# A shared expert's second product with its weights standing and 512 tokens moving, turned back in the final sums

## The chip, the cores and the metric

The kernel runs on one core of a Trainium2 chip. The metric is device time in microseconds (us), the median of several runs. PE is TensorE, DVE VectorE, ACT ScalarE, POOL GpSimd, and SP the engine whose queue issues most of the DMAs. An f32 matmul shows in the profile as two instructions.

## The reference

The input x has 8 sequences of 512 tokens with 128 features. A layer norm modulated by a conditioning vector is followed by four Mamba2 layers and a residual sum with a gate; a second modulated layer norm is followed by a mixture of experts. Only the mixture matters here:

```python
normed = hidden_states * rsqrt(mean(hidden_states**2) + 1e-08) * norm_weight
shared = maximum(normed @ sw1 + sb1, 0.0) @ sw2 + sb2     # 128 -> 512 -> 128, all tokens
...                                                       # 8 experts of that size, 2 a token
return shared + routed
x = x + gb * ffn(h)                                       # gb: one row of 128 a sequence
```

## The kernel before, in words

The first two thirds are the Mamba layers. While the last scan steps drain, streams of small steps are merged by a planner (`arrange`, L724): every step names an engine, a cost in us, what it needs and gives, and a PSUM bank that it takes or drops; the planner picks the step that could start first, and the order in which it picks them is the order in every engine's queue. The streams are the scan's lanes, the routing of four sets of two sequences (`rejoin`, L372), the rows' scatter into lists by expert (`send`), the shared expert's products on PE (`shared_products`, L595) and its evictions on ACT (`shared_copies`, L621), and the first 17 tiles of the routed experts.

The shared expert works by sequence b. Four first products (L601) have a block of `sw1` as weights and the sequence's 512 tokens, features on the partitions, moving; each fills a bank and leaves it with bias and relu (L632) as a part of `hds[b]`, hidden units on the partitions. The second product (L613) has 128 tokens of `hds` as weights and a block of `sw2` moving, so that its result has tokens on the partitions: for each of four token blocks s four products over the hidden units k add up in a quarter of one bank. Each s is one planner step of cost 0.9. A copy on ACT (L636) puts the bank into `accs[b]`, which lies in a tile of the Mamba layers' states (shown as `h`).

The routed experts then go through 39 tiles of 256 rows, the last 22 of them in a loop written out by hand: load weights and rows of tile j+3 (`fetch`), hidden products of tile j+1 (L1563), turn of tile j+2 (L1551), second products of tile j (`combine`, L1581), weighing (`weigh_results`, L1593 and L1595 on DVE), scatter of the results into `yg` (L562). Every pass of this loop also takes two steps of the folds. `fold(b)` has four: load the gate row `gb` to all partitions (L1510, SP's queue), add the bias `b2` to `accs[b]` (L1512), multiply by `gb` (L1514), add to `xs[b]`, the residual (L1516).

When the last scatter is done, two rows a token are read back from `yg` on SP's and ACT's queues (L1709). For each sequence PE adds both in a bank by products with the identity as weights (L1715, L1716), DVE multiplies by `gb` (L1718) and adds to `xs[b]` (L1721), and SP stores the result (L1722).

Of the kernel before, what the change touches and what calls it, by code (L numbers as in the profile page):

```python
# [8 lines left out]
F32 = mybir.dt.float32  # L9
I32 = mybir.dt.int32  # L10
AF = mybir.ActivationFunctionType
# [4 lines left out]
P = 128  # L16
# [38 lines left out]
def adaln_mamba_moe(  # L55
# [27 lines left out]
    nc = tc.nc  # L83
    B, L, DM = x.shape
# [4 lines left out]
    NC = L // Q  # L89
# [4 lines left out]
    FK = FH // P  # L94
# [39 lines left out]
    ident = const.tile([P, P], F32, name="ident")  # L134
# [115 lines left out]
    hTs, hp, xp, xs = {}, {}, {}, {}  # L250
# [3 lines left out]
    fp = ctx.enter_context(tc.tile_pool(name="fp", bufs=1))  # L254
# [4 lines left out]

    rwT = fp.tile([P, E], F32, name="rwT")  # L260
    b1 = fp.tile([P, E1, FK], F32, name="b1")
    b2 = fp.tile([P, DM], F32, name="b2")
    rank = fp.tile([P, E], F32, name="rank")
    below = fp.tile([P, P], F32, name="below")
    base = fp.tile([P, E], F32, name="base")
# [25 lines left out]
    def prepare_experts(pool):  # L291

        pm = pbank("pmods")
        nc.tensor.matmul(pm[:B, : 4 * DM], sc, wm[:, 2 * DM :], start=True, stop=True)
        pv = pm[:B, : 4 * DM].rearrange("p (k d) -> p k d", d=DM)
        mod, mag = (pool.tile([P, NH, Q], F32, tag="dV", name=n)[:, :4, :DM] for n in ("mod", "mag"))
        yield
        nc.scalar.activation(mag[:B, :2, :], pv[:, 0:4:3, :], AF.Abs)
        nc.scalar.copy(mod[:B, 1, :], pv[:, 1, :])
        nc.scalar.activation(mod[:B, 2, :], pv[:, 2, :], AF.Copy, bias=1.0)  # L300
        nc.vector.tensor_scalar(mag[:B, 2:, :], pv[:, 0:4:3, :], 0.0, 2.0, ALU.is_ge, ALU.mult)

        nc.gpsimd.iota(rank, pattern=[[-1, E]], base=E, channel_multiplier=0, **exact)
        nc.gpsimd.iota(base, pattern=[[ER, E]], base=0, channel_multiplier=0, **exact)
        yield
        nc.vector.tensor_scalar_max(mag[:B, :2, :], mag[:B, :2, :], 0.25)
        for k in range(2):
            nc.vector.scalar_tensor_tensor(
                mod[:B, 3 * k, :], mag[:B, 2 + k, :], -1.0, mag[:B, k, :], ALU.add, ALU.mult
            )  # L310
        nc.gpsimd.tensor_sub(below, upto, ident)
        nc.gpsimd.iota(tok, pattern=[[L, 2], [1, NC]], base=0, channel_multiplier=NC, **exact)
        yield
        nc.vector.tensor_mul(mod[:B, 0, :], mod[:B, 0, :], fw[:B])
        yield
        nc.sync.dma_start(mods, mod[:B])
        yield
        with nc.allow_non_contiguous_dma(reason="small parameters, laid out once"):
            nc.sync.dma_start(rwT, router_w.rearrange("e d -> d e"))
            nc.sync.dma_start(b1[:, :E, :], eb1.rearrange("e (k p) -> p e k", p=P))  # L320
            nc.sync.dma_start(b1[:, E, :], sb1.rearrange("(k p) -> p k", p=P))
        nc.sync.dma_start(b2, sb2.partition_broadcast(P))
        yield

    hTx = {}
# [27 lines left out]
    def one(engine, cost):  # L353
        return ((engine, cost),)
# [227 lines left out]
    def pbank(name):  # L582
        pool, tag = pools[pick[0]], "p"
        if spare:
            pool, tag = spare[0]
            spare.append(spare.pop(0))
        return pool.tile([P, 512], F32, tag=tag, name=name)


    accs, w12 = {}, []  # L590

    home = {b: g for g, seqs in enumerate(sets) for b in seqs}
    hds, phs, pes = {}, {}, {}

    def shared_products():  # L595

        for b in range(B + 1):
            for k in range(FK if b < B else 0):
                yield one("PE", 0.87), (("routed", home[b]), ("weights", 0)), ("ph", b, k), ("ph", b, k), None
                phs[b, k] = ph = pbank(f"phs{b}_{k}")  # L600
                nc.tensor.matmul(ph[:, :L], w12[0][:, k * P : (k + 1) * P], hTx[b], start=True, stop=True)  # L601
            for s in range(NC if b else 0):
                yield (
                    one("PE", 0.9),
                    (("hidden", b - 1),),
                    ("pe", b - 1) if s == NC - 1 else None,
                    ("pe", b - 1) if s == 0 else None,
                    None,
                )
                if s == 0:  # L610
                    hd, pes[b - 1] = hds.pop(b - 1), pbank(f"pes{b - 1}")
                for k in range(FK):
                    nc.tensor.matmul(  # L613
                        pes[b - 1][:, s * DM : (s + 1) * DM],
                        hd[:, k, s * P : (s + 1) * P],
                        w12[1][:, k * P : (k + 1) * P],
                        start=(k == 0),
                        stop=(k == FK - 1),
                    )

    def shared_copies():  # L621

        for b in range(B + 1):
            for k in range(FK if b < B else 0):
                needs = (("ph", b, k),)
                if k == 0 and b < XB:
                    needs = (("ph", b, k), ("out", (NL * B - XB + b + 1) * NC - 1))
                yield one("ACT", 0.69), needs, ("hidden", b) if k == FK - 1 else None, None, ("ph", b, k)
                if k == 0:
                    hds[b] = xbp.tile([P, NX, L], F32, tag="xbc", name=f"hds{b}")  # L630
                ph = phs.pop((b, k))
                nc.scalar.activation(hds[b][:, k, :], ph[:, :L], AF.Relu, bias=b1[:, E, k : k + 1])  # L632
            if b:
                yield one("ACT", 0.6), (("pe", b - 1),), None, None, ("pe", b - 1)
                accs[b - 1] = hp[(b - 1) // 2][:, (b - 1) % 2]
                nc.scalar.copy(accs[b - 1].rearrange("p s d -> p (s d)"), pes.pop(b - 1))  # L636

    tab, done = {}, []

# [113 lines left out]
    with ExitStack() as actx:  # L753
# [530 lines left out]
        for t in range(-NC * LEAD - EARLY, TAIL):  # L1284
            p = t + NC * LEAD
# [23 lines left out]
            u, s = divmod(t, NC)  # L1309
# [194 lines left out]
    gbs = {}  # L1504
    fgb = ctx.enter_context(tc.tile_pool(name="fgb", bufs=B))

    def fold(b):

        gbs[b] = fgb.tile([P, DM], F32, tag="gb", name=f"gb{b}")
        nc.sync.dma_start(gbs[b], mods[b, 3].partition_broadcast(P))  # L1510
        yield
        nc.vector.tensor_add(accs[b], accs[b], b2.unsqueeze(1).to_broadcast([P, NC, DM]))  # L1512
        yield
        nc.vector.tensor_mul(accs[b], accs[b], gbs[b].unsqueeze(1).to_broadcast([P, NC, DM]))  # L1514
        yield
        nc.vector.tensor_add(xs[b], xs[b], accs[b])  # L1516

    xts, w1x, w2x, b2x, rows_in, hdx, pts, pxs, ys = ({} for _ in range(9))

# [151 lines left out]
    def hidden(j):  # L1671
        pick[0] = "P"
        for half in range(2):
            hidden_product(j, half)
            hidden_relu(j, half)

    with tc.manual_schedule():
        for js in ((J0, J0 + 1), (J0 + 2,)):
            for rest in [fetch(j) for j in js]:
                rest()  # L1680
        for j in (J0, J0 + 1):
            turn(j)
            turned_copy(j)
        hidden(J0)
        folding = [fold(b) for b in range(B)]
        for j in range(J0, NT):
            if j + 3 < NT:
                fetch(j + 3)()
            if j + 1 < NT:
                hidden(j + 1)  # L1690
            if j + 2 < NT:
                turn(j + 2)
                turned_copy(j + 2)
            pick[0] = "D"
            combine(j)
            weigh_results(j)
            send_results(j)
            for _ in range(2):
                if folding and not step(folding[0]):
                    del folding[0]  # L1700

        pick[0] = "P"
        y1, y2 = {}, {}
        for b in range(B):
            both = xbp.tile([P, NX, L], F32, tag="xbc", name=f"y{b}") if b % 2 == 0 else both
            for c, (eng, y) in enumerate(((nc.sync, y1), (nc.scalar, y2))):
                y[b] = both[:, 2 * (b % 2) + c, :]
                r = c * T + b * L
                eng.dma_start(  # L1709
                    y[b].rearrange("p (s d) -> p s d", d=DM),  # L1710
                    yg[r : r + L, :].rearrange("(p s) d -> p s d", s=NC),
                )
        for b in range(B):
            sum2 = pbank(f"sum{b}")
            nc.tensor.matmul(sum2, ident, y1[b], start=True, stop=False)  # L1715
            nc.tensor.matmul(sum2, ident, y2[b], start=False, stop=True)  # L1716
            y = y1[b].rearrange("p (s d) -> p s d", d=DM)
            nc.vector.tensor_mul(  # L1718
                y, sum2.rearrange("p (s d) -> p s d", d=DM), gbs[b].unsqueeze(1).to_broadcast([P, NC, DM])
            )  # L1720
            nc.vector.tensor_add(xs[b], xs[b], y)  # L1721
            nc.sync.dma_start(out[b].rearrange("(s p) d -> p s d", p=P), xs[b])  # L1722
# [51 lines left out]
```

## Time and profile before

| what | value |
|---|---|
| median of 3 runs | 1024.13 us (1022.54 to 1024.15) |
| the profiled execution's own time | 1026.45 us |
| its span, first to last instruction | 1024.7 us |
| PE busy | 907.9 us, 89% |
| DVE, ACT, POOL busy | 80%, 75%, 81% |
| mean granted TensorE clock | 0.952 |
| first products of the shared expert (L601) | 64 instructions, 739.6 to 830.1 us |
| second products (L613) | 256 instructions, 748.4 to 837.6 us |
| copies of their results (L636) | 8, median 0.586 us |
| folds (L1512, L1514, L1516) | 3 x 8, 0.683, 0.683 and 0.692 us, 913.5 to 974.0 us |
| final sums (L1715, L1716) | 32 instructions, from 1003.3 us |

The profile gives instructions by line, engine and tile. Its first block cuts the span into 40 slices and shows each engine's busy tenths; its chain of waits goes back from the last instruction to what released it. PE's instructions are pipelined, so that their durations overlap: an instruction's real share of the time is seen from the chain, where a group's length is divided by its count. PEld are the weight loads, which run beside the products.

### The profile page before, as it was taken

The numbers are of one execution on the slowest core, as the hardware profiler recorded it, in microseconds if no ns is written. First come the engines' busy times: TensorE is split into PE (matmuls) and PEld (weight loads), VectorE is DVE, ScalarE is ACT, GpSimd is POOL, SyncE is SP. The second block draws the span as 40 slices with busy tenths as digits, with TensorE's granted clock in tenths as the row PEclk, the third lists the DMA queues.
The fourth block names the chain that finished last, engine by engine and source line by source line (L and its number), as shares of the span: only waits on it lengthen the run. The fifth ranks groups of instructions, "written<-read, shape, count | busy, mean of one in ns | idle before, by whom it ended". The sixth has DMA issues, their size and how long they took to land.

```text
span 1024.7 us, 21895 instructions
## 1 busy us (share of the span) xinstructions
PE 907.9 (89%) x7284; PEld 677.1 (66%) x7284; DVE 821.4 (80%) x2012; ACT 767.1 (75%) x1765; POOL 831.5 (81%) x847
## 2 busy tenths in 40 slices
PE   4669899999999999999999999777687999999976
PEld 2336676676777666777767677566455678888862
DVE  3879989899999899999899999687765665457744
ACT  4897899999999999999999989864585533333320
POOL 8768899999999999999999999676868775445550
PEclk9888999999999999999999999998787899999997
DMA  6142455665766656653434434540011257778737
GB/s 124 5 157 69 149 168 159 184 184 177 201 198 186 180 170 187 186 175 119 141 114 135 134 115 141 181 152 25 32 32 44 69 151 209 217 220 230 226 113 246
DMA packets 134304, 151.23 MB, mean 148 GB/s; under 512 B 22568, under 2 KB 106696, under 8 KB 134192
## 3 DMA queue, kind: packets, MB, share of 16 engines
q1 hardware_dynamic: 127184, 137.91, 45.2%
q0 software_dynamic: 4672, 9.42, 2.7%
q10 hardware_dynamic: 2336, 2.50, 0.8%
q8 instruction: 58, 0.95, 0.4%
q14 instruction: 54, 0.44, 0.1%
HBM read 120.07 MB, written 29.71 MB: 146 GB/s over the span
## 4 chain that ended last, share of the span: by engine, by line
PE 45%; ACT 17%; POOL 16%; DVE 9%; DMA 7%; issue 5%; SPq 1%; POOLq 0%; ACTq 0%; DVEq 0%
PE pe L1581 5%; POOL dV L1022 5%; PE px L839 4%; PE ph L1563 4%; PE py L1163 4%; DMA rows<-xg 3%; PE po L1216 3%; PE pz L844 3%; PE py L1153 3%; POOL dV L1030 3%; PE phs L601 3%; PE py L1101 2%; PE py L1110 2%; POOL xd L1077 2%; ACT xbc L873 2%
## 5 line engine op out<-in xcount | busy, mean ns | idle before, releaser
L860 DVE SCALAR_TENSOR_TENSOR xbc<-px,cw,xbc 128x511 f32<-128x511 f32 (+2 forms) x384 | 284.1, 741 | 13.1 <-ACT xbc L850 10.1
L1022 POOL TENSOR_TENSOR dV<-dV,cum 128x1024 f32<-128x1024 f32 (+1 forms) x128 | 232.5, 1817 | 7.6 <-DMA dV<-crow 7.4
L1092 DVE TENSOR_TENSOR dV<-dV,ptx 128x1024 f32<-128x1024 f32 x128 | 155.2, 1213 | 17.9 <-ACT xT L1070 11.4
L1030 POOL TENSOR_SCALAR_AFFINE_SELECT dV<-dV 128x1024 f32<-128x1024 f32 x128 | 141.1, 1102 | 1.2
L562 POOL DMA_INDIRECT yg<-y,ix x78 | 81.0, 1038 | 68.7 <-DVE y L1595 52.2
L1077 POOL TENSOR_TENSOR xd<-xT,dt 128x512 f32<-128x512 f32 (+1 forms) x128 | 120.6, 942 | 18.2 <-ACT xT L1070 17.8
L1043 ACT ACTIVATE dV<-dV 128x1024 f32<-128x1024 f32 (+1 forms) x128 | 129.2, 1010 | 3.7 <-POOL dV L1030 3.3
L850 ACT ACTIVATE xbc<-px,cbias,cw 128x512 f32<-128x512 f32 x128 | 100.0, 782 | 6.3 <-PE px L839 5.4
L839 PE MATMUL px<-hT,Wi 128*128 128x512 f32 x192 | 99.5, 600 | 0.0
L1101 PEld LDWEIGHTS py<-xbc,st 128*128 128x128 f32 x384 | 57.1, 195 | 61.9 <-issue 25.5
L1574 ACT ACTIVATE hd<-ph,bs 128x256 f32<-128x256 f32 x78 | 32.8, 471 | 80.1 <-PE ph L1563 79.2
L1216 PE MATMUL po<-Wo,g 128*128 128x128 f32 x512 | 89.2, 297 | 0.0
L562 POOL DMA_INDIRECT xg<-row,ix x64 | 63.5, 993 | 27.0 <-issue 16.1
L1163 PE MATMUL py<-dV,xd 128*32 128x128 f32 x2048 | 83.8, 282 | 0.0
L1153 PEld LDWEIGHTS py<-xbc,dg 128*128 128x128 f32 x512 | 76.4, 195 | 5.2
L1153 PE MATMUL py<-xbc,dg 128*128 128x128 f32 x512 | 79.8, 279 | 0.0
L1216 PEld LDWEIGHTS po<-Wo,g 128*128 128x128 f32 x512 | 69.1, 196 | 13.1 <-issue 12.9
L1110 PE MATMUL py<-xd,xT 128*128 128x256 f32 x192 | 61.1, 401 | 16.6 <-issue 8.1
L1581 PE MATMUL pe<-w,hd 128*128 128x128 f32 x624 | 75.7, 275 | 0.0
L1563 PE MATMUL ph<-xt,w 128*128 128x256 f32 x312 | 73.9, 380 | 1.4 <-ACT xt L1555 1.4
L1101 PE MATMUL py<-xbc,st 128*128 128x128 f32 x384 | 61.3, 283 | 13.6 <-DVE rg L1223 6.8
L1581 PEld LDWEIGHTS pe<-w,hd 128*128 128x128 f32 x624 | 72.7, 192 | 0.1
(264 smaller groups left out, 2225.2 us busy)
## 6 DMA issues: line engine op xcount, KB each, us to landing
dV<-crow SPq DMA_DIRECT2D x128, 512.0 KB
w<-in_L_ffn_ew_dram SPq DMA_DIRECT2D x78, 256.0 KB
xg<-blank SPq DMA_DIRECT2D x64, 260.0 KB
ecum<-crow SPq DMA_DIRECT2D x256, 48.0 KB
rows<-xg SPq DMA_DIRECT2D x39, 130.0 KB
b<-in_L_ffn_eb_dram SPq DMA_DIRECT2D x39, 64.0 KB
x<-in_L_attn_x_dram SPq DMA_DIRECT2D x8, 256.0 KB
md<-mods SPq DMA_DIRECT2D x8, 256.0 KB
```

Source lines behind the costliest of these rows:

```text
L562: i = nc.gpsimd.indirect_dma_start(out=to, out_offset=bass.IndirectOffsetOnAxis(ap=ix, axis=0), in_=of, in_offset=None)
L839: nc.tensor.matmul(px[v, k][:, :L], Wi[l][:, c0 : c0 + P], hT[v], start=True, stop=True)
L860: nc.vector.scalar_tensor_tensor(xbc[v][:, k, d:], px[v, k][:, : L - d], cw[:, l, k, KT - 1 - d : KT - d], xbc[v][:, k, d:], ALU.mult, ALU ...
L1022: nc.gpsimd.tensor_tensor(dV[i][:, :w], dV[i][:, :w], cums[g][:, h0 : h0 + w].unsqueeze(2).to_broadcast([P, w, Q]), ALU.subtract,)
L1030: nc.gpsimd.affine_select(out=dV[i], in_=dV[i], pattern=[[0, NH], [1, Q]], compare_op=ALU.is_ge, fill=-1e30, base=0, channel_multiplier=-1,)
L1043: nc.scalar.activation(dV[i][:, :w], dV[i][:, :w], AF.Exp)
L1077: nc.gpsimd.tensor_mul(xds[i][:, :w], xv.unsqueeze(1).to_broadcast([P, w, NH, HD]), dts[g][:, :w, h0 : h0 + NH].unsqueeze(3).to_broadcast( ...
L1092: nc.vector.tensor_mul(Ms[i], Ms[i], pg.pop(i).unsqueeze(1).to_broadcast([P, NH, Q]))
L1101: nc.tensor.matmul(py[i][:, k, :], st[i - 1][:, k * P : (k + 1) * P], xbc[u][:, NB + 1, t], start=(k == 0), stop=True, skip_group_check=True,)
L1153: nc.tensor.matmul(py[i][:, k, :], dg[l][:, k, :], xbc[u][:, k, t], start=False, stop=True, skip_group_check=True,)
L1216: nc.tensor.matmul(pp[:, c * DM : (c + 1) * DM], g[:, k, :], Wo[l][:, k, :], start=(k == 0), stop=(k == NB - 1))
L1581: nc.tensor.matmul(pe[:, s, :], hd[:, k, s * P : (s + 1) * P], w2[:, k, :], start=(k == 0), stop=(k == FK - 1))
```

## The change

The second product of the shared expert swaps its operands. A block of `sw2` is the weights, and a part k of the hidden tile moves, 512 tokens at once; four such products add up over a whole bank. The result has features on the partitions and tokens along the free axis. The bias `sb2` is then one value a partition, and is added in the eviction, which becomes an activation (Identity with a bias). `fold(b)` keeps only the load of the gate row. In the final sums the result is turned back: four products a sequence, each with 128 tokens of `accs[b]` as weights and the identity moving, open the bank to which the two identity products of before add the routed rows. The turns of sequences 0 and 1 stand ahead of the first sum, and those of b+2 behind the sum of b.

```diff
-    b2 = fp.tile([P, DM], F32, name="b2")
+    b2 = fp.tile([P, 1], F32, name="b2")
...
-        nc.sync.dma_start(b2, sb2.partition_broadcast(P))
+        nc.sync.dma_start(b2, sb2.rearrange("(p o) -> p o", o=1))
...
-            for s in range(NC if b else 0):
+            for k in range(FK if b else 0):
                 yield (
                     one("PE", 0.9),
                     (("hidden", b - 1),),
...
-                for k in range(FK):
-                    nc.tensor.matmul(
-                        pes[b - 1][:, s * DM : (s + 1) * DM],
-                        hd[:, k, s * P : (s + 1) * P],
-                        w12[1][:, k * P : (k + 1) * P],
-                        start=(k == 0),
-                        stop=(k == FK - 1),
-                    )
+                nc.tensor.matmul(
+                    pes[b - 1][:, :L],
+                    w12[1][:, k * P : (k + 1) * P],
+                    hd[:, k, :],
+                    start=(k == 0),
+                    stop=(k == FK - 1),
+                )
...
-                accs[b - 1] = hp[(b - 1) // 2][:, (b - 1) % 2]
-                nc.scalar.copy(accs[b - 1].rearrange("p s d -> p (s d)"), pes.pop(b - 1))
+                accs[b - 1] = hp[(b - 1) // 2][:, (b - 1) % 2].rearrange("p s d -> p (s d)")
+                nc.scalar.activation(accs[b - 1], pes.pop(b - 1), AF.Identity, bias=b2)
...
         nc.sync.dma_start(gbs[b], mods[b, 3].partition_broadcast(P))
         yield
-        nc.vector.tensor_add(accs[b], accs[b], b2.unsqueeze(1).to_broadcast([P, NC, DM]))
-        yield
-        nc.vector.tensor_mul(accs[b], accs[b], gbs[b].unsqueeze(1).to_broadcast([P, NC, DM]))
-        yield
-        nc.vector.tensor_add(xs[b], xs[b], accs[b])
...
+        def shared_rows(b):
+            sums[b] = pbank(f"sum{b}")
+            for s in range(NC):
+                nc.tensor.matmul(
+                    sums[b][:, s * DM : (s + 1) * DM], accs[b][:, s * P : (s + 1) * P], ident, start=(s == 0), stop=False
+                )
+
+        for b in range(2):
+            shared_rows(b)
         for b in range(B):
-            sum2 = pbank(f"sum{b}")
-            nc.tensor.matmul(sum2, ident, y1[b], start=True, stop=False)
+            sum2 = sums[b]
+            nc.tensor.matmul(sum2, ident, y1[b], start=False, stop=False)
             nc.tensor.matmul(sum2, ident, y2[b], start=False, stop=True)
+            if b + 2 < B:
+                shared_rows(b + 2)
```

More of the change, by code (lines that the diff above doesn't have):

```diff
@@ L605, in shared_products @@
                     (("hidden", b - 1),),
-                    ("pe", b - 1) if s == NC - 1 else None,
-                    ("pe", b - 1) if s == 0 else None,
+                    ("pe", b - 1) if k == FK - 1 else None,
+                    ("pe", b - 1) if k == 0 else None,
                     None,
                 )
-                if s == 0:
+                if k == 0:
                     hd, pes[b - 1] = hds.pop(b - 1), pbank(f"pes{b - 1}")
-                for k in range(FK):
-                    nc.tensor.matmul(
-                        pes[b - 1][:, s * DM : (s + 1) * DM],
-                        hd[:, k, s * P : (s + 1) * P],
-                        w12[1][:, k * P : (k + 1) * P],
-                        start=(k == 0),
-                        stop=(k == FK - 1),
-                    )
+                nc.tensor.matmul(
[5 more added lines that the diff above has]
+                )
     def shared_copies():
@@ L1712, in adaln_mamba_moe @@
                 )
+        sums = {}
+        def shared_rows(b):
[6 more added lines that the diff above has]
+            shared_rows(b)
         for b in range(B):
-            sum2 = pbank(f"sum{b}")
-            nc.tensor.matmul(sum2, ident, y1[b], start=True, stop=False)
+            sum2 = sums[b]
+            nc.tensor.matmul(sum2, ident, y1[b], start=False, stop=False)
             nc.tensor.matmul(sum2, ident, y2[b], start=False, stop=True)
+            if b + 2 < B:
+                shared_rows(b + 2)
             y = y1[b].rearrange("p (s d) -> p s d", d=DM)
```

## The prediction

> **What bounds the kernel now.** I read the page first, for where TensorE (PE) is full, then the chain of waits piece by piece for the three stretches that the change touches, then the waits and the busy time by windows inside each.
>
> ```profile
> PE   4669899999999999999999999777687999999976
> PEclk9888999999999999999999999998787899999997
> ```
>
> A slice is 25.6 us. PE is full to about 640 us, thins out while the scan drains, the rows are routed and the shared expert runs (739 to 838 us), is full again through the routed experts (839 to 993 us), and ends in a short tail. The change takes work from the second and third stretch and puts work into the last. The chain of waits at the end of the shared expert:
>
> ```profile
> 823.04 2.68 PE pes L613 x24
> ...
> 827.28 3.44 PE phs L601 x8
> 830.72 7.16 PE pes L613 x64
> ```
>
> Columns are start, length, instruction and count; an f32 matmul is two instructions. A first product (L601, 512 columns moving) costs 3.44/8 = 0.430 us an instruction, a second product (L613, 128 columns) 7.16/64 = 0.112 us. The time follows the columns: 4 x 0.112 = 0.448 against 0.430. The stretch of routed experts, by windows before, during and after the folds:
>
> ```profile
> 860.00:910.00 50.00, 47.69 (x322) 42.83 (x322) 25.03 (x87) 15.87 (x37) 24.90 (x26) 1.00 0.74 214
> 910.00:976.00 66.00, 63.46 (x438) 57.33 (x437) 47.82 (x140) 22.12 (x51) 36.92 (x32) 1.00 0.79 226
> 976.00:993.00 17.00, 16.27 (x117) 15.03 (x116) 9.07 (x33) 4.78 (x11) 7.90 (x10) 1.00 0.44 126
> ```
>
> The second number is the window's length, the third PE's busy time, the fifth VectorE's (DVE). DVE goes from 50% to 72% where the folds run, and PE stays at 95%, 96%, 96%: PE paces this stretch with and without them. The tail by the chain:
>
> ```profile
> 998.84 4.43 DMA y<-yg
> 1003.32 2.08 PE sum L1715 x2
> 1005.40 1.71 PE sum L1716 x2
> ...
> 1018.26 0.86 PE sum L1715 x2
> 1019.12 0.87 PE sum L1716 x2
> 1020.01 0.70 DVE y L1718
> 1020.74 0.69 DVE x L1721
> ```
>
> Once the first rows have landed, every piece is PE until 1019.99. The waits from 994 us on say the same, seen from DVE, and show the free gap ahead:
>
> ```profile
> DVE y L1718 <- PE sum L1716: 15.6, 8, 12.7
> ...
> PE sum L1715 <- DMA y<-yg: 9.8, 1, 9.8
> ```
>
> DVE waits for PE before each of its 8 products; PE waits for a load once, 9.8 us, before the first sum, and never again. PE's granted clock is the third number from the right here:
>
> ```profile
> 998.00:1000.00 2.00, 0.00 (x0) 0.00 (x0) 0.00 (x0) 0.00 (x0) 0.00 (x0) 0.61 0.28 53
> ...
> 1003.00:1004.00 1.00, 0.68 (x1) 0.50 (x2) 0.00 (x0) 0.00 (x0) 0.00 (x0) 0.50 0.96 348
> ...
> 1008.00:1009.00 1.00, 1.00 (x2) 0.33 (x2) 0.56 (x1) 0.00 (x0) 0.00 (x0) 0.65 1.06 397
> 1009.00:1010.00 1.00, 1.00 (x4) 0.44 (x3) 0.29 (x1) 0.00 (x0) 0.00 (x0) 1.00 1.05 393
> ```
>
> The gap halves the clock near 998.4, and it is whole again near 1008.7, so the tail's first 5.4 us run at half speed.
>
> **The change, part by part.**
>
> *Second product.* Per batch 16 matmuls of 128 columns become 4 of 512: 32 instructions of 0.112 us (3.58) become 8 of 0.430 us (3.44), 0.14 us less. Columns streamed stay 2,048, and the full clock is granted wherever L613 runs. Five of the eight groups lie on the chain of waits (at 768, 798, 823 to 827, and two from 830.7); behind the other three PE sits idle for 1.5 us or more, waiting for the routing. So I take 5 x 0.14 = 0.7 us gained, bounds 0 and 8 x 0.14 = 1.1. The steps for the planner keep their number (4), engine, cost (0.9), needs and bank, so its order stays; the new products could also start on a first part of the hidden tile, but they stand behind later first products anyway.
>
> The Trainium skill speaks for the change here: "TensorE: Matmul & The Clock Gate", section "Back-to-back issue gap", gives about 81 ns a matmul at 128 columns and 131 ns at 512 in a stream of weight loads and matmuls. As an estimate from that page, 256 x 0.081 = 20.7 us would become 64 x 0.131 = 8.4, five eighths of the difference is 7.7 us, and with 48 x 0.081 = 3.9 us in the tail and 0.2 for the evictions the sum would be a gain of 3.6 us. Both figures lie under this trace's 112 and 430 ns, and their ratio of 1.6 stands against 3.8; the trace decides.
>
> *Eviction.* The copy (L636, 0.586 us) becomes an activation with a bias. The nearest row is L632, same shape, from PSUM, with a bias: 0.687. The chain passes the copy twice: at 802.29, where the next set's squares queue behind it on ScalarE, and at 837.96, where the first routed tile's turned copy does, with PE waiting. 2 x 0.1 = 0.2 us lost, bounds 0 and 8 x 0.1 = 0.8.
>
> *Folds.* 24 DVE passes of 0.68 to 0.69 us (16.5 us) go. Nobody waits on the chain for them: L1593 starts within a microsecond or two of the products that it reads, and the 16 tiles with folds (L1593 at 912.60 to 976.11) take 3.97 us each, the 14 before (845.43 to 900.45) 3.93. I take nothing. At most, PE's waits for rows in that stretch go (0.41 + 1.01 + 0.98 = 2.4 us at 914.7, 942.4 and 966.1); but the stretch before has such waits too (0.72, 0.66, 0.56), without folds. What is late next there is PE itself, at 3.73 us a tile where it never waits (L1593 at 892.91 and 896.64, for one). The 8 loads of gb (64 KB each, 0.43 us to issue on SP's queue) remain, one per tile instead of one every second; SP issues its loads about two tiles ahead, and nothing but those loads queues behind. The bias load moves from 64 KB to 512 bytes early on SP's queue, hidden by 700 us.
>
> *Final sums.* Per batch 4 matmuls of 128 x 128, 8 instructions, each with weights of its own. The row with that shape and that change of weights is L1581, on the chain at 3.59/32 = 0.112 us, so 8 x 0.112 = 0.9 us a batch; from below 0.430/4 = 0.107 by the columns of L601, from above 0.112 + 0.192 = 0.304 if no weight load overlapped (the mean weight load of L1581). I take L1581, where the loads overlap. Batches 0 and 1 need only what lay ready since 838 us and banks whose last reader ended by 991, so they run from 993.5 to 995.3, inside the 9.8 us wait: free, and if that cover were gone they would cost 1.8. The other six stand between the sums, where PE never waits: 6 x 0.9 = 5.4 us, bounds 5.2 and, unoverlapped, 14.6. PE's extra wait is for a bank: batch b+2's turn needs the bank of sum b-1, read by DVE 0.3 + 0.7 us after that sum, while PE needs 1.7 us for sum b; so it waits for nothing, and only the next sums queue behind it.
>
> *Clock in the tail.* The half-speed time is a stretch of time, not of work: what is added lands at full clock behind it. PE's gap shrinks to 8.0 us, and the clock fell 4.9 us into the gap, so it falls again. Rise and fall are 3 x 3.4 us apart, as if in steps of 3.4; a start at another point of a step moves the rise by up to 1.7 us either way, worth half of it, 0.85 us.
>
> *Sum.* 5.4 - 0.7 + 0.2 = +4.9 us. The profiled execution took 1026.45 (span 1024.7 and 1.75 around it) and would take 1031.3. It lies 2.3 above the median of 1024.13, so on the runs I add the same: **1029.0**.
>
> **The rivals.**
>
> *Faster: the second product was held by its weight loads.* L613 has 256 loads of 0.192 us, 49 us in all, and only 64 remain. If the new passes took no more than a 256-column one (L1563, 1.73/8 = 0.216 us), a group would fall from 3.58 to 1.73, five groups save 9.2 us, and 5.4 + 0.2 - 9.2 = -3.6 gives 1020.5. It decides once a pass is under (5 x 3.58 - 5.6 - 2.0)/40 = 0.26 us. Against: L601 is that very shape, and takes 0.430.
>
> *No change: the tail hides it.* If the early turns of batches 0 and 1 held the clock up past 1003.3, the half-speed loss of 5.4/2 = 2.7 us would go: 4.9 - 2.7 = +2.2, 1026.3, and with the folds' 2.4 us gained on top -0.2, 1023.9. For it: 1.8 us more of work sits in the gap. Against: 8.0 us without work remain, and the clock fell after 4.9.
>
> *Much slower: weight loads in the tail don't overlap.* 48 x 0.304 = 14.6 in place of 5.4 gives +14.1, 1038.2. Against: L1581 and the old L613 alternate loads and passes in the same way at 0.112.
>
> *It doesn't do what it says.* If the planner placed the new products elsewhere, the routing would shift; its inputs are equal, so I give this nothing of its own.
>
> **How the numbers follow.** My forecast 0.86, faster 0.04, no change 0.07, much slower 0.03. A difference of 0.2% is 2.05 us, about what a measurement of this kernel can tell from no change. The forecast's own range: below, 5.2 - 1.1 - 0.85 = 3.2, and half of the folds' 2.4 off, 2.0: 1026.1; above, 5.4 + 0.85 + 0.8 = 7.1: 1031.2. That range leaves out most of the rivals' 0.14 and a little more, so I keep it. A hundredth of the forecast's chance falls under 2.05 us. Slower 0.88, same 0.08, faster 0.04.
>
> **What would show it.** Right: L613 as 64 instructions at 0.43 us on the chain; the three fold lines gone and tiles still near 3.95 us apart; 16 short instructions near 994; PE without a gap from the first sum to the last, that stretch 22.0 us long instead of 16.7; nothing between the last sum and the end changed. Wrong: PE waiting within the sums for loads or banks (the tail had another bound), the last routed product well before 992 us (the folds cost more than nothing), passes of L613 under 0.4 us, or full clock at the first sum.

## The result, and the profile after

The changed kernel took 1029.21 us (median of 11 runs, 1026.81 to 1034.88), the one before, run beside it, 1024.62 (11 runs): ratio 1.0047, 95% interval 1.0027 to 1.0067, or 2.8 to 6.9 us more. The forecast was 1029.0 and slower. Its profiled execution took 1031.35 us, span 1029.6; the sum had said 1031.3.

Later runs fell on several chips. On two of those the kernel before took some 30 us more and the changed kernel some 23, and there the changed kernel was level or faster (0.9982 and 0.9968). That is the part nobody had forecast; it has a section of its own.

The chain of waits at the end of the shared expert, after (start, length, instruction and count):

```profile
822.02 2.58 PE pes L612 x6
...
826.13 3.43 PE phs L601 x8
829.56 6.88 PE pes L612 x16
```

A second product is now 8 instructions in 3.44 us, where it was 32 in 3.58: 0.430 us a pass, as a first product. The routed stretch by windows (length, then busy time of PE, weight loads, DVE, ACT, POOL, then clock, DMA share, GB/s):

```profile
860.00:910.00 50.00, 47.28 (x324) 42.92 (x323) 24.80 (x88) 15.62 (x36) 24.98 (x27) 1.00 0.78 219
910.00:976.00 66.00, 63.70 (x441) 58.09 (x440) 33.84 (x118) 22.30 (x51) 30.92 (x33) 1.00 0.80 227
```

The folds are gone from DVE (33.84 us in the second window, 47.82 before), and PE is busy for 63.70 us of 66 instead of 63.46. The tail by the chain:

```profile
998.38 4.32 DMA y<-yg
1002.74 2.08 PE sum L1720 x2
1004.82 1.71 PE sum L1721 x2
1006.52 1.71 PE sum L1712 x8
1008.23 0.95 PE sum L1720 x2
...
1020.48 0.89 PE sum L1712 x8
...
1023.95 0.87 PE sum L1721 x2
1024.85 0.70 DVE y L1725
```

L1712 are the turns (8 instructions a sequence). PE has no hole from 1002.74 to 1024.82, 22.08 us against 16.67 before: 5.41 more, with 5.4 forecast. The turns of one sequence take 0.89 us, those in the half-speed part 1.71. From 996 us on DVE still waits for PE before each product, and PE for a load once:

```profile
DVE y L1725 <- PE sum L1721: 20.9, 8, 12.5
...
PE sum L1720 <- DMA y<-yg: 7.9, 1, 7.9
```

### The profile page after: what moved, and what is told of

Read it like the earlier page. It is cut to its first block, busy times and chain, and to the rows that moved or that the text cites. A ratio compares the mean times of both kernels' runs of the same rounds, so it can differ in the third digit from the quotient of the medians.

```text
span 1029.6 us, 21609 instructions
## 1 busy us (share of the span) xinstructions
PE 914.0 (89%) x7156; PEld 667.0 (65%) x7156; DVE 807.0 (78%) x1988; ACT 767.2 (75%) x1765; POOL 824.6 (80%) x847
## 4 chain that ended last, share of the span: by engine, by line
PE 49%; ACT 17%; POOL 13%; DVE 8%; DMA 7%; issue 4%; SPq 1%; POOLq 0%; DVEq 0%; ACTq 0%
PE px L838 5%; PE pe L1575 5%; PE py L1162 4%; PE po L1215 4%; POOL dV L1021 4%; PE ph L1557 4%; DMA rows<-xg 3%; PE pz L843 3%; PE py L1152 3%; PE py L1100 3%; PE py L1109 3%; PE phs L601 2%; POOL dV L1029 2%; DVE dV L1091 2%; ACT xbc L872 2%
## 5 line engine op out<-in xcount | busy, mean ns | idle before, releaser
L562 POOL DMA_INDIRECT yg<-y,ix x78 | 74.6, 957 | 75.7 <-DVE y L1589 58.9
```

Of the source, the lines that this page charges most:

```text
L562: i = nc.gpsimd.indirect_dma_start(out=to, out_offset=bass.IndirectOffsetOnAxis(ap=ix, axis=0), in_=of, in_offset=None)
```

## The experiments

Durations of the tail run from the start of the first sum to the end of the last, in the profiled execution. Repeated runs of one kernel lie 5 to 14 us apart, so a term under 2 us is read from the trace, and the ratio only bounds the whole.

**No turns.** The two early calls and the one behind the sums are out.

```diff
-        for b in range(2):
-            shared_rows(b)
...
-            if b + 2 < B:
-                shared_rows(b + 2)
```

> The changed kernel without the 32 turns: the shared expert's result is computed and evicted and left out of the output. If PE paces the tail, all of the loss goes: the stretch from the first sum to the last falls from 22.1 to 16.7 us and the time to 0.5 us under that of the kernel before, 0.9995 of it. Rival, the loss came from elsewhere (the routed stretch without its folds, or the clock): the time stays 2 us or more over the kernel before.

Ratio 0.9981 (0.9959 to 1.0004). The chain of its tail begins and ends with

```profile
1003.05 2.08 PE sum L1718 x2
...
1019.13 0.87 PE sum L1719 x2
```

which is 16.95 us. With the turns out the loss is out, and nothing of it stays elsewhere: the rival's 2 us lie outside the interval.

**No folds.** The kernel before without its 24 DVE passes.

```diff
-        nc.vector.tensor_add(accs[b], accs[b], b2.unsqueeze(1).to_broadcast([P, NC, DM]))
...
-        nc.vector.tensor_mul(accs[b], accs[b], gbs[b].unsqueeze(1).to_broadcast([P, NC, DM]))
...
-        nc.vector.tensor_add(xs[b], xs[b], accs[b])
```

> The kernel before without the 24 DVE passes of the folds: the old second product runs, and its result is left out of the output. If PE paces the routed tiles, they stay 3.9 to 4.0 us apart and the time stays within 0.5 us of the kernel before. Rival, the folds delayed loads or scatters: up to 2.4 us less. Against the kernel that leaves out the turns, which differs from this one by the second product and its eviction alone, I expect PE's products of the shared expert 1.1 us longer in all and the time 0.5 us longer.

Ratio 0.9987 (0.9970 to 1.0004); tiles 3.98 us apart between 912.17 and 975.91 (L1590), where they were 3.97 with folds. So the trace shows no cost of the folds in the routed tiles; the ratio alone would not exclude the rival's 2.4 us, since its interval reaches down to 3.1 us less. The 0.5 us between this kernel and the last is not to be seen in their ratios; in the trace the second products' groups differ by 3.58 to 3.44, as forecast.

**All turns late.** Each turn stands behind its own two identity products.

```diff
-        for b in range(2):
-            shared_rows(b)
...
-            nc.tensor.matmul(sum2, ident, y2[b], start=False, stop=True)
-            if b + 2 < B:
-                shared_rows(b + 2)
...
+            nc.tensor.matmul(sum2, ident, y2[b], start=False, stop=False)
             for s in range(NC):
                 nc.tensor.matmul(
...
+                    sum2[:, s * DM : (s + 1) * DM], accs[b][:, s * P : (s + 1) * P], ident, start=False, stop=(s == NC - 1)
+                )
```

> The changed kernel with each sequence's turn behind its two identity products, so that none runs in the gap. If PE paces the tail and the gap covered two turns for nothing, the tail from the first sum to the last is 8 x 0.9 = 7.2 us longer than before, 23.9 us, and the time 1.8 us over the changed kernel, 6.6 over the one before. Rival, the early turns gained or lost something besides (the clock, banks): the tail is 22 us, or over 25.

Ratio 1.0069 (1.0044 to 1.0095), 7.1 us by the ratio; the tail 23.69 us. Against the changed kernel that is 1.61 us for the two turns that had lain in the gap (1.8 less a rise of the clock at another point): the cover was worth what the sum said.

**Filler in the gap.** The kernel before, 8 throwaway products ahead of the sums.

```diff
+        fill = pbank("fill")
+        for k in range(8):
+            nc.tensor.matmul(fill, ident, hp[k // 2][:, k % 2].rearrange("p s d -> p (s d)"), start=True, stop=True)
```

> The kernel before with 8 more identity products of 512 columns in PE's gap, into a bank that nobody reads. They end near 1000.4 and leave less than 3 us without work. If the half speed at the start of the tail comes from the gap, the clock stays whole, the tail's 16.7 us fall to 13.8 and the time by 2.7 us, ratio 0.9973. Rival, the half speed comes from something else (the loads that arrive at that time), or the loads pace the sums as soon as PE is fast: the tail stays at 16 us or more.

A miss: ratio 0.9999 (0.9982 to 1.0017), tail 15.51 us, 1.2 saved and not 2.7. The windows show why (PE's busy time is the third number, the granted clock the third from the right):

```profile
1004.00:1006.00 2.00, 1.37 (x4) 0.30 (x2) 0.00 (x0) 0.00 (x0) 0.00 (x0) 1.00 0.57 106
1006.00:1007.00 1.00, 0.00 (x0) 0.00 (x0) 0.00 (x0) 0.00 (x0) 0.00 (x0) 1.00 0.91 350
1007.00:1008.00 1.00, 0.00 (x0) 0.00 (x0) 0.00 (x0) 0.00 (x0) 0.00 (x0) 0.93 1.05 404
1008.00:1009.00 1.00, 0.77 (x1) 0.50 (x2) 0.00 (x0) 0.00 (x0) 0.00 (x0) 0.50 1.02 363
...
1011.00:1012.00 1.00, 1.00 (x4) 0.50 (x3) 0.25 (x1) 0.00 (x0) 0.00 (x0) 0.86 0.83 293
```

2.9 us without work were enough: the clock fell near 1007.9 and came back near 1011.3, one step of 3.4 us.

**Filler up to the loads.** The same with 11 products, against the kernel with 8.

```diff
-        for k in range(8):
-            nc.tensor.matmul(fill, ident, hp[k // 2][:, k % 2].rearrange("p s d -> p (s d)"), start=True, stop=True)
+        for k in range(11):
+            nc.tensor.matmul(fill, ident, hp[k % 4][:, k % 2].rearrange("p s d -> p (s d)"), start=True, stop=True)
```

> The kernel before with 11 throwaway identity products of 512 columns instead of 8, 9.4 us of work in a gap of 9.8. If the half speed comes from the gap, the clock stays whole, the tail is 13.8 us instead of 16.7 and the time 2.7 us less, ratio 0.9973: then the gain of the eight early turns with filler is the clock's and not the standing weights'. Rival, the clock falls in any gap or falls for another reason: the tail stays at 15.5 us or more.

PE's gap is 0.6 us, the clock stays whole, the tail is 14.0 us and the ratio 0.9979 (0.9954 to 1.0004). The half speed comes from the gap; that the whole run gains by it is not told from noise.

**Eight early turns**, with the sums in all eight PSUM banks, which belong to three pools (three of P, two of the turns' pool T, three of D):

```diff
-        for b in range(2):
+        for b in range(B):
             shared_rows(b)
...
-            if b + 2 < B:
-                shared_rows(b + 2)
```

> The changed kernel with all eight turns ahead of the first sum, in eight banks. They take 7.2 us of PE's gap and end near 1000. If PE alone paces the tail and the gap covers what runs in it, the six turns' 5.4 us go from the tail, and what is left of the half speed decides the rest: the kernel before with 8 filler products had the clock fall after 2.7 us without work and lost 1.5 us, so 13.8 to 16.7 us from the first sum to the last, and the time 0 to 3 us under the kernel before, 5 to 8 under the changed one. Rival, the loads pace the sums once PE is quicker: the sums wait for loads and the tail stays over 16.5 us.

Ratio 1.0008 (0.9984 to 1.0033), tail 15.71 us, and no wait for loads within it. The six turns' 5.4 us are gone; after 2.55 us of gap the clock fell again, at 999.5, just behind the start of the first sum.

**Eight early turns behind three throwaway ones**, so that PE has work until the first rows land, against the eight early turns.

```diff
...
+        for b in range(3):
+            shared_rows(b, True)
         for b in range(B):
             shared_rows(b)
```

> The same with three throwaway turns (2.7 us) ahead of the eight, so that PE has work until the first rows land. If the half speed comes from the gap alone, the clock stays whole, the tail is 8 x 1.72 = 13.8 us and the time 3 us under the kernel before, ratio 0.997, and 7.5 us under the changed kernel. Rival, the loads pace the sums: PE waits within the tail, which stays at 15 us or more.

The chain runs through PE without a hole, from the turns into the sums:

```profile
990.81 9.83 PE sum L1718 x88
1000.64 1.02 PE sum L1728 x2
...
1013.68 0.87 PE sum L1729 x2
```

Tail 13.9 us, the 13.8 forecast. The ratio, 0.9991 (0.9969 to 1.0014), is not told from one, nor from the 0.997 expected.

**The old second product with its sums opened early**, by one product of 512 columns a sequence; DVE still adds the bias, and the other two passes of each fold are out.

```diff
-        nc.vector.tensor_mul(accs[b], accs[b], gbs[b].unsqueeze(1).to_broadcast([P, NC, DM]))
-        yield
-        nc.vector.tensor_add(xs[b], xs[b], accs[b])
...
         for b in range(B):
...
+            nc.tensor.matmul(sums[b], ident, accs[b].rearrange("p s d -> p (s d)"), start=True, stop=False)
```

> The kernel before with the old second product, the bias still added by DVE, and the other two passes of each fold replaced by one product of 512 columns a sequence with the identity as weights, all eight ahead of the first sum in eight banks. 8 x 0.86 = 6.9 us in the gap: the same tail as with eight early turns, within 1.7 us for the point at which the clock falls, and a time within 2 us of that kernel, at most 0.5 us of it from the second product. Rival, the standing weights are worth more than 0.7 us: this one is 2 us or more slower than the eight early turns.

Tail 15.71 us, the very length of the eight early turns. The ratio is 1.0029 (0.9999 to 1.0060), the median 2.7 us over theirs, as the rival had it; but the intervals overlap, and the tail shows no such difference. What the standing weights are worth beyond 0.14 us a group is not settled here.

**The changed kernel with filler**, 9 products ahead of its two early turns, and **two repeats**, of the changed kernel, one of them beside it and beside a repeat of the 11 products on one chip:

```diff
+        fill = pbank("fill")
+        for k in range(9):
+            nc.tensor.matmul(fill, ident, hp[k % 4][:, k % 2].rearrange("p s d -> p (s d)"), start=True, stop=True)
         for b in range(2):
             shared_rows(b)
```

> The changed kernel with 9 throwaway identity products of 512 columns (7.7 us) ahead of the two early turns, so that PE has work until the first rows land. If the turns cost PE's time at whatever clock, the tail is 13.8 + 5.4 = 19.2 us with a whole clock, and the time is 2.7 us over the kernel before and 2 to 3 under the changed kernel. Rival, the turns' cost came in part from the half speed: the tail is under 18 us.

> The changed kernel once more, on the chip of the two beside it: 4.6 us over the kernel before, ratio 1.0045, the tail 21 to 23 us by where the clock's rise falls.

> The kernel before with the 11 throwaway products once more, for an interval: ratio 0.9975, the tail 13.8 us. Rival, the gain seen was chance: ratio within 0.001 of one.

> The changed kernel a third time, since on the chip before both kernels took some 30 us more, with a pause of 12 to 20 us behind the shared expert in which PE, VectorE and ScalarE got an instruction only every 0.7 us or so, and the changed kernel was not slower there. If the loss is the tail's, then without such a pause the ratio is 1.0045 and the tail 21 to 23 us, and with the pause the tail is the same and the ratio between 0.996 and 1.002. Rival, the loss seen first was chance: without a pause the ratio is under 1.002.

The tails came out as expected: 19.4, 22.1, 14.0 and 22.1 us, in the order of the four expectations. The times did not:

| kernel | median, us | before beside it | ratio |
|---|---|---|---|
| changed, filled | 1050.59 | 1055.09 | 0.9963 (0.9936 to 0.9989) |
| changed again | 1052.98 | 1055.09 | 0.9982 (0.9964 to 1.0000) |
| before, 11 products | 1053.89 | 1055.09 | 0.9990 (0.9968 to 1.0011) |
| changed, third (another chip) | 1051.87 | 1055.82 | 0.9968 (0.9951 to 0.9986) |

## Two chips on which the sign turns

On these two chips the routed experts start late. Behind the shared expert, the timeline of the changed kernel's third run shows (idle time before an instruction, and what ended it, in brackets; "remote" is another core or an unknown queue):

```profile
842.44 1.99 PE L1557 MATMUL ph<-xt,w 128*128 128x256 f32 x8 [1.85 <-issue]
...
853.15 0.84 ACT L1568 ACTIVATE hd<-ph,bs 128x256 f32<-128x256 f32 x2 [10.76 <-remote]
...
854.41 3.78 PE L1557 MATMUL ph<-xt,w 128*128 128x256 f32 x8 [9.97 <-ACT hd L1568]
```

The products were ready near 844, and ScalarE took them up at 853.15; VectorE stood still for 13.8 us, and PE for 10. In the old form, before with 11 products, such a stretch caught PE among its second products:

```profile
850.77 0.27 PE L613 MATMUL pes<-ws,hds 128*128 128x128 f32 x1 [1.04 <-issue]
...
852.20 0.37 PE L613 MATMUL pes<-ws,hds 128*128 128x128 f32 x1 [1.16 <-issue]
...
853.62 0.37 PE L613 MATMUL pes<-ws,hds 128*128 128x128 f32 x1 [1.06 <-issue]
```

From 847.9 to 863.5 us PE went through 11 passes and the weight loads between them, one pass in 1.4 us instead of one in 0.112, ended by "issue": PE waited for nothing that the profile shows. The first sum starts at 1023.6 to 1024.2 in the three profiles of the changed product and at 1036.3 in the one of the old, which is that of the slowest of its 12 runs.

These passes carry the smaller part of those 12 us. Already the last first product (L601) started at 841.9 in the old form and at 831.8 to 832.7 in the three others. The old form's profile has an earlier stop, behind the second of its eight second products, which had ended near 774.5:

```profile
781.86 0.59 ACT L636 COPY h<-pes 128x512 f32<-128x512 f32 x1 [10.05 <-remote]
781.95 0.23 DVE L534 TENSOR_TENSOR rest<-pos,base 128x64 f32<-128x64 f32 x1 [8.46 <-remote]
```

In the three others that eviction came at once, at 771.7 to 771.9, and only the next one was late, after 3.2 to 5.7 us in which ScalarE stood still. By the medians, the third run gains 4.0 us in spite of 5.4 lost in the tail, so some 9 us come from ahead of the tail.

Shown is that the tail's loss is the same on these chips (19.4 us with filler against 14.0), that PE, ScalarE, VectorE and SP's queue start instructions late there, with no engine named that held them, while GpSimd keeps its pace of one scatter in 1.27 us, and that the first sum comes 12 us earlier with the new product, in one profile of the old form against three. That the cause is the number of instructions (256 passes and as many weight loads became 64 and 64) is argued, not shown: no kernel was run there that changed this number alone, and what slows the issue stays open. So does whether the earlier stop belongs to the old product or to that one run.

## Why the prediction was right, and where it would not have been

*Second product:* 0.14 us a group forecast, 3.58 to 3.44 measured; the steps kept their places, with the product for the positions still between the third and fourth step. The term rests on a stream that is issued without a pause, a condition that wasn't named. On the two chips above the gain ahead of the tail was far larger; that it is the second product's is not shown. The rival that forecast faster had that sign, but by a pass under 0.26 us, and a pass took 0.430.

*Eviction:* 0.682 us (mean of L635) against 0.581, the 0.1 forecast.

*Second product and eviction together:* the first sum came 0.58 us earlier, at 1002.74 instead of 1003.32, where -0.7 and +0.2 had said 0.5. That fit is luck. The first product of the shared expert had started 2.0 us earlier (737.6, before 739.6), ahead of every second product, and from there to the first sum the changed kernel took 265.1 us, the one before 263.7. One profile each doesn't resolve terms of this size; nor does a median that is 0.2 us off the forecast, with an interval of 4 us.

*Folds:* nothing forecast; removal alone left the tiles at 3.98 us, and the ratio's interval ends at -3.1 and +0.4 us.

*Final sums:* 0.89 us a turn with 0.9 forecast, 5.41 in all with 5.4. The kernel without turns lost it, the one with all turns late paid for the two that had been covered, and the filled one kept 19.4 - 14.0 = 5.4 at a whole clock: the price does not hang on the half speed. The second rival needed a whole clock at the first sum, and it was 0.50 there. The bank wait did not come, and weight loads overlapped, which excludes the much slower case.

*Clock:* that the early turns don't hold it up was right, the reason half so. The clock had fallen 4.9 us into the gap, and I took that as the time a gap needs. It is not one. In the changed kernel (granted clock third from the right):

```profile
996.00:998.00 2.00, 0.00 (x0) 0.00 (x0) 0.00 (x0) 0.00 (x0) 0.96 (x1) 1.00 0.20 66
998.00:1000.00 2.00, 0.00 (x0) 0.00 (x0) 0.00 (x0) 0.00 (x0) 0.00 (x0) 0.51 0.24 44
```

The last turn ended near 994.8 and the clock fell at 998.0, after 3.2 us; with 8 filler products after 2.5.

The Trainium skill, "TensorE: Matmul & The Clock Gate", section "Why this matters for your kernels", warns of idle gaps over about 3 us between bursts. The runs agree that a gap lowers the clock, and put the safe length lower: it fell after gaps of 2.5 to 2.9 us and held after 0.6 and 1.0.

## What to carry to other kernels

Here, swapping the operands of an f32 product kept the columns that stream through PE, and with them its time (3.44 us a group for 3.58); what a change moves into a stretch where PE is the only one that others wait for, it pays in full. The same eight turns cost 5.4 us with six of them between the sums and nothing with all eight in the idle gap ahead of them, given banks to hold the results. A difference of half a per cent should be run on more than one chip before it is believed to have one sign.

## What the runs showed of the hardware

PE's granted clock falls to 0.50 and comes back after a multiple of about 3.4 us: after 10.2 us in the kernel before and in the changed one (998.46 to 1008.70, 998.05 to 1008.29), after 3.4 with 8 filler products, with eight early turns and with the old product's sums opened early (1007.86 to 1011.28, 999.52 to 1002.93, 1006.95 to 1010.37). How long PE has been idle does not set the fall: from the last work to the fall were 5.0, 3.2 and 2.5 us in three kernels (993.50 to 998.46, 994.81 to 998.05, 1005.37 to 1007.86). With the old product's sums opened early the clock even fell after the sums had begun: their first instruction pair took 0.96 us at 1005.75, and the pair from 1008.17 1.71 us.

The runs read as if a fall went by whether a step of 3.4 us was mostly without work. Counted back from the falls, the step that ended there held 0 to 1.2 us of work in these five kernels, and a step with 1.9 us, in the kernel before, left the clock whole. For the rise that is not enough: in the changed kernel the step from 1001.5 to 1004.9 held 2.1 us of work at half clock, and the clock rose a step later. No run was made to test this reading.

The kernel before took 1024.6 to 1026.3 us (median) on some chips and 1055.1 and 1055.8 on two others, though PE's clock was granted in full through the routed stretch on both (1.00 from 838 to 990 us before, and from 870 to 1025 us with the 11 products on the slower chip).
